# Cross attention of an encoder-decoder layer: VectorE's sums and GpSimd's product of a normalization put in separate slots

## The chip, the core and the metric

The kernel runs on one core of a Trainium2 chip. The metric is the device time of one execution in microseconds (us). Everything is float32. The engines are named as the profile names them: PE (TensorE matmuls), PEld (its weight loads), DVE (VectorE), ACT (ScalarE), POOL (GpSimd) and SP (SyncE, which here only issues DMAs).

## The reference

One encoder layer works on a short context (2 sequences of 77 tokens), and one decoder layer on 2 sequences of 2048 tokens. The width is 512, with 16 heads of 32 and a feed-forward width of 2048. What the change touches is the decoder's cross attention, and what lies beside it is the decoder's feed-forward layer.

```
def _mha(xq, xkv, w_in, b_in, w_out, b_out, bias):
    ...
    scores = jnp.einsum('bhqd,bhkd->bhqk', q, k) / jnp.sqrt(jnp.asarray(hd, xq.dtype))
    scores = scores + bias[None]
    attn = jax.nn.softmax(scores, axis=-1)
    out = jnp.einsum('bhqk,bhkd->bhqd', attn, v)
    ...
    return out @ w_out.T + b_out
...
y = y + _mha(yn, yn, dec_sa_in_w, ...)                       # causal self attention
y = y + _mha(_ln(y, ...), memory, dec_ca_in_w, ..., cb)      # cross attention: 77 keys
h = _ln(y, dec_n3_s, dec_n3_b)
y = y + (jax.nn.relu(h @ dec_ff1_w.T + dec_ff1_b) @ dec_ff2_w.T + dec_ff2_b)
```

## The kernel before

The 4096 decoder rows are cut into eight blocks of 512 tokens (two batches of four), and each block into four query tiles of 128 tokens. The order of the instructions on every engine is written out by hand. No scheduler moves anything: an engine takes its own queue in the order in which the program issues it, and semaphores make it wait for other engines.

The first part of the span (to about 1780 us) is the encoder and the causal self attention of all blocks, with the cross attention of the first block worked in (`first_cross`). In the second part (from about 1780 us to the end) the loop goes over the blocks' feed-forward layers. Each block has 56 slots: 28 for the first weight matrix and 28 for the second. Both products are done by a scheme of seven block products (`PARTS`, `ORDER`) instead of eight, whose operands are sums and differences of quarters of the matrices. Each of the seven takes four slots.

A slot is `ff_slot(s)`. It first calls `prepare(s + 3)`, which builds the operands of the slot three later, and then issues the product of slot s itself (`first_product`, L1132, or `second_product`, L1161). In the first layer POOL builds the sums of weight quarters (L1115, `vv<-pp`) into a ring of four buffers, and sums of activations (`oT<-nT`). In the second layer DVE builds one of the two operands (also L1115). After a product DVE adds it into the result (L1147), and ACT applies the relu (L1150).

While the loop does the feed-forward layer of block x, a generator `cross(x + 1)` issues the cross attention of the next block, one step of a list called `plan` per slot. The step stands ahead of the slot's own `ff_slot`. There are seven such blocks, x = 0 to 6. Query tile t starts at slot 14 + 7t, and its stages are placed at fixed distances from that start:

- `score`: 16 matmuls (L766), then on DVE for each of four groups of heads the maximum (L775) and its subtraction (L776). In the first block of a batch the bias is added ahead of these for tiles 0 and 1 (L773). One of the seven, at about 2280 us in the profile, has this.
- `exp`: one exponential on ACT over 16 x 77 values per row (L779).
- `normalize`: DVE's sum (L784) and reciprocal (L785), and POOL's product of the probabilities with the reciprocals (L786).
- `turned`: 16 transposes on PE (L792), with copies to SBUF on DVE and ACT (L794, L796).
- `times_v`: 16 small matmuls (L803) and a copy on ACT (L807).
- `out`: four matmuls (L812) and DVE's addition into the residual (L813).

For tiles 1 to 3 the six stages stand at distances 0, 2, 3, 6, 9 and 11 from the tile's start. For tile 0 the first three stand one slot earlier, at -1, 1 and 2. So tile 0's score is issued ahead of slot 13, its exponential ahead of slot 15, its normalization ahead of slot 16, and its transposes ahead of slot 20.

Of the kernel before, what the change touches and what calls it, by code (L numbers as in the profile page):

```python
# [54 lines left out]
def tile_encoder_decoder(ctx: ExitStack, tc: tile.TileContext, ins, out):  # L55
# [5 lines left out]
    def wchunk(name, c0, n=D):  # L61

        return ins[name][:, c0 : c0 + n].rearrange("(c p) o -> p c o", p=P)
# [85 lines left out]
    with (  # L149
# [20 lines left out]
        def bank():  # L170

            i = count["bank"] % count["banks"]
            count["bank"] += 1
            return psum[:, i, :]
# [6 lines left out]
        def rows4(r):  # L181
            return slice(r * HD, (r + 1) * HD)
# [571 lines left out]
        def attend_stages(q, kTc, v, y, biased, pr, pts, place, w_o, bi=None):  # L754


            prh = pr.rearrange("p (h k) -> p h k", k=S)
            by_r = pr.rearrange("p (g r k) -> p g r k", r=HC, k=S)
            keep = {}

            def score():
                mx = sm.tile([P, NC, HC], F32, name="cmx", tag="cmx", bufs=3)
                banks = [bank() for _ in range(HC)]
                for g in range(NC):
                    for r in range(HC):
                        nc.tensor.matmul(  # L766
                            banks[r][:, ts(g, S)], q(g)[rows4(r)], kTc[rows4(r), g, :], start=True, stop=True
                        )
                for r in range(HC):
                    s = banks[r][:, : NC * S].rearrange("p (g k) -> p g k", k=S)  # L770
                    d = by_r[:, :, r, :]
                    if biased:
                        nc.vector.tensor_tensor(d, s, bi[r] if bi else d, ALU.add)  # L773
                        s = d
                    nc.vector.tensor_reduce(mx[:, :, r], s, AX.X, ALU.max)  # L775
                    nc.vector.tensor_tensor(d, s, mx[:, :, r, None].to_broadcast([P, NC, S]), ALU.subtract)  # L776

            def exp():
                nc.scalar.activation(pr, pr, AF.Exp)  # L779

            def normalize():
                su = sm.tile([P, H], F32, name="csu", tag="csu", bufs=2)
                ri = sm.tile([P, H], F32, name="cri", tag="cri", bufs=2)
                nc.vector.tensor_reduce(su, prh, AX.X, ALU.add)  # L784
                nc.vector.reciprocal(ri, su)  # L785
                nc.gpsimd.tensor_tensor(prh, prh, ri[:, :, None].to_broadcast([P, H, S]), ALU.mult)  # L786

            def turned():
                for g in range(NC):
                    pt = bank()  # L790
                    for r in range(HC):
                        nc.tensor.transpose(pt[:S, ts(r, P)], prh[:, g * HC + r, :], ident)  # L792
                    if g % 2:
                        nc.vector.tensor_copy(pts(g), pt[:S, :])  # L794
                    else:
                        nc.scalar.copy(pts(g), pt[:S, :])  # L796

            def times_v():
                ot = bank()
                for g in range(NC):  # L800
                    for r in range(HC):
                        h = g * HC + r
                        nc.tensor.matmul(  # L803
                            ot[rows4(r), ts(g, P)], v[:, ts(h, HD)], pts(g)[:, ts(r, P)], start=True, stop=True
                        )
                keep["oT"] = place()
                nc.scalar.copy(keep["oT"], ot)  # L807

            def out():
                mm, oT = bank(), keep["oT"]  # L810
                for c in range(NC):
                    nc.tensor.matmul(mm, oT[:, ts(c, P)], w_o[:, c, :], start=(c == 0), stop=(c == NC - 1))  # L812
                nc.vector.tensor_tensor(y(), mm, y(), ALU.add)  # L813

            return score, exp, normalize, turned, times_v, out

        def first_cross():


            plan = {}  # L820

            def at(slot, f):
                plan.setdefault(slot, []).append(f)

            o = 2 * HC * MB
            ys = [pp[:, o + t * D : o + (t + 1) * D] for t in range(TB)]
            qT = pp[:, o + 2048 : o + 4096].rearrange("p (g n) -> p g n", n=MB)
            prs = [pp[:, o + 4096 + i * H * S : o + 4096 + (i + 1) * H * S] for i in range(2)]
            o += 4096 + 2 * H * S
            kTc = pp[:, o : o + NC * S].rearrange("p (c k) -> p c k", k=S)  # L830
            vc = pp[:S, o + NC * S : o + NC * S + D]
            slab = pp[:, o + NC * S + D : o + NC * S + 2 * D].rearrange("p (c n) -> p c n", n=P)
            assert o + NC * S + 2 * D <= 12288
            nT = pp[:, HC * MB : 2 * HC * MB].rearrange("p (c n) -> p c n", n=MB)
            wq, wo = vv[:, 8:12, :], vv[:, 12:16, :]
            rows = {"dec_ca_out_b": kT[:, 0, 3 * MB :], "dec_ff2_b": kT[:, 3, 3 * MB :]}
            oT, xn = kT[:, 1, 3 * MB :], kT[:, 2, 3 * MB :]

            def pts(g):
                return kT[:S, g, 2 * MB : 3 * MB]  # L840

            def loads():
                for t in range(TB):
                    nc.sync.dma_start(ys[t], y1[0][0][:, t, :])
                for n, row in rows.items():
                    i = _ROWS.index(n)
                    nc.sync.dma_start(row, ins["rows"][i : i + 1, :].to_broadcast([P, D]))
                nc.sync.dma_start(wq, wchunk("dec_ca_in_wT", 0))
                nc.sync.dma_start(kTc, ckT_d[:, :, :S])
                nc.sync.dma_start(vc, cv_d[:, 0, :])  # L850

            def more_loads():
                for i in range(2):
                    bias_tile(prs[i].rearrange("p (h k) -> p h k", k=S), 2, P, S, 255 - P * i)
                nc.sync.dma_start(wo, wchunk("dec_ca_out_wT", 0))

            at(0, loads)
            at(5, more_loads)
            for t in range(TB):
                y = lambda t=t: ys[t]  # L860
                fs = norm_stages(
                    y, "n2", rows["dec_ca_out_b"], lambda: xn, lambda t=t: nT[:, :, ts(t, P)]
                )
                for k, f in enumerate(fs):
                    at(1 + t + k, f)
            for g in range(NC):
                at(7 + g, lambda g=g: q_group(g, wq[:, :, ts(g, P)], nT, qT[:, g, :]))
            for t in range(TB):
                y = lambda t=t: ys[t]
                fs = attend_stages(  # L870
                    lambda g, t=t: qT[:, g, ts(t, P)], kTc, vc, y, t < 2, prs[t % 2], pts, lambda: oT, wo
                )
                for k, f in zip((0, 1, 2, 4, 5, 6), fs):
                    at(11 + 3 * t + k, f)
                fs = norm_stages(y, "n3", rows["dec_ff2_b"], lambda: xn, lambda: slab)
                for k, f in enumerate(fs):
                    at(18 + 3 * t + k, f)

                def store(t=t):
                    nc.sync.dma_start(nT3_d[:, :, ts(t, P)], slab)  # L880
                    nc.sync.dma_start(y1[0][0][:, t, :], ys[t])

                at(20 + 3 * t, store)
            return plan
# [307 lines left out]
        def cross(x):  # L1192
# [9 lines left out]
            for t in range(TB):  # L1202
                fs = norm_stages(
                    lambda t=t: y_of(x, t), "n2", bv, place("xt"), lambda t=t: nT2[:, :, ts(t, P)]
                )
# [11 lines left out]
            for t in range(TB):  # L1217
                at = 14 + 7 * t
                y = lambda t=t: y_of(x, t)
                biased = m == 0 and t < 2  # L1220
                fs = attend_stages(
                    lambda g, t=t: qT[g // 2][:, g % 2, ts(t, P)], kTcs[b], vcs[b][:S, :], y, biased, pr,
                    lambda g: pts_all[:S, g, :], place("xr"), wbt,
                    bias_1 if biased and t else None,
                )

                for k, f in zip((0 if t else -1, 2 if t else 1, 3 if t else 2, 6, 9, 11), fs):
                    plan[at + k].append(f)
                fs = norm_stages(y, "n3", bo, place("xt"), lambda t=t: nTt[:, :, ts(t, P)])
                for k, f in zip((13, 15, 17), fs):  # L1230
                    plan[at + k].append(f)
# [129 lines left out]
```

## Time and profile before

| What | us |
|---|---|
| Time, median of 3 runs | 2927.04 (2926.18 to 2927.46) |
| The profiled execution, its own time | 2926.58 |
| Its span, first to last instruction | 2924.8 |
| PE busy in the span | 2866.0 (98%) |
| DVE busy | 2096.9 (72%) |
| ACT busy | 1303.8 (45%) |
| POOL busy | 744.8 (25%) |
| Mean granted TensorE clock | 0.990 |

The profile is of one execution. A row of a timeline gives the start in us, the duration in us, the engine, the line and operation, the output and inputs with their shapes, the number of instructions merged into the row, and in square brackets how long the engine was idle before it and whose work ended that. A row of waits gives who waited for whom, the total in us, the number of times and the longest. A row of the table of stretches gives, for a stretch of the span, the busy time and count of PE, PEld, DVE, ACT and POOL, then the granted PE clock (PEclk, 1.00 is full), the DMA share and GB/s. PE works on a float32 matmul in two passes, and the trace counts each: four matmuls show as x8.

### The profile page before, as it was taken

What the parts mean: (1) busy time and instruction counts of PE and PEld (TensorE: products, weight loads), DVE (VectorE), ACT (ScalarE), POOL (GpSimd) and SP (SyncE); (2) the same over time, 40 slices, a digit from 0 to 9 for tenths busy, and PEclk for the clock granted to TensorE, in tenths of its full rate; (3) what the DMA queues carried; (4) which work ended last, traced back from release to release, by engine and by line L of the source; (5) the groups of instructions that cost most, each with busy time, mean ns of one, the idle gap of its engine ahead of it and who ended that gap; (6) DMA issues with size and microseconds to landing.
All of it is one profiled execution on the core that took longest, in us unless ns stands there. A gap on an engine that the chain in (4) does not pass through costs nothing.

```text
span 2924.8 us, 60785 instructions
## 1 busy us (share of the span) xinstructions
PE 2866.0 (98%) x24440; PEld 2018.7 (69%) x24440; DVE 2096.9 (72%) x5951; ACT 1303.8 (45%) x2431; POOL 744.8 (25%) x601
## 2 busy tenths in 40 slices
PE   8899999999999999999999999999999999999999
PEld 5557666666666556666666667777777777777788
DVE  4767688888987788888888894646474756565645
ACT  3344456546665445565566673323232323232321
POOL 0100000000000101000000004565656464646464
PEclk9899999999999999999999999999999999999999
DMA  6413301201111502211201115000001000000000
GB/s 176 98 54 112 100 16 54 65 16 45 34 41 60 141 19 73 73 30 48 56 16 37 41 39 198 1 30 1 29 1 47 1 29 1 30 1 30 1 15 15
DMA packets 117837, 137.11 MB, mean 47 GB/s; under 512 B 18433, under 2 KB 73265, under 8 KB 117427
## 3 DMA queue, kind: packets, MB, share of 16 engines
q1 hardware_dynamic: 117554, 133.22, 15.5%
q8 instruction: 192, 3.15, 0.4%
q14 instruction: 91, 0.74, 0.1%
HBM read 111.33 MB, written 21.86 MB: 46 GB/s over the span
## 4 chain that ended last, share of the span: by engine, by line
PE 86%; DVE 11%; issue 1%; ACT 1%; DMA 1%; POOL 0%; SPq 0%; DVEq 0%; POOLq 0%; ACTq 0%
PE psum L1161 13%; PE psum L1132 13%; PE psum L411 12%; PE psum L361 10%; PE psum L428 7%; DVE pp L370 5%; PE psum L206 4%; PE psum L812 4%; PE psum L751 4%; PE psum L230 4%; PE psum L242 4%; PE psum L217 3%; DVE pp L377 3%; PE psum L792 2%; PE psum L766 1%
## 5 line engine op out<-in xcount | busy, mean ns | idle before, releaser
L387 ACT ACTIVATE pp<-pp,nm 128x128 f32<-128x128 f32 (+15 forms) x512 | 614.1, 1210 | 197.7 <-DVE nm L384 194.9
L370 DVE TENSOR_SCALAR_CACHE_REDUCE pp<-psum 128x512 f32<-128x512 f32 (+3 forms) x1024 | 557.9, 589 | 53.5 <-PE psum L361 51.5
L411 PE MATMUL psum<-ident,pp 128*128 128x128 f32 x4352 | 547.9, 279 | 17.6 <-DVE mx L377 11.7
L411 PEld LDWEIGHTS psum<-ident,pp 128*128 128x128 f32 x4352 | 474.2, 142 | 130.3 <-DVE pp L370 56.5
L417 ACT COPY pts<-psum 128x512 f32<-128x512 f32 (+3 forms) x592 | 298.6, 577 | 516.9 <-PE psum L411 390.9
L1115 POOL TENSOR_TENSOR vv<-pp 128x512 f32<-128x512 f32 x320 | 425.3, 1345 | 148.6 <-PE psum L1132 128.5
L361 PE MATMUL psum<-kT,q 32*128 32x512 f32 (+3 forms) x2560 | 351.8, 579 | 8.2 <-DVE mx L377 4.0
L415 DVE COPY pts<-psum 128x512 f32<-128x512 f32 (+2 forms) x544 | 329.7, 659 | 40.7 <-PE psum L411 38.9
L428 PEld LDWEIGHTS psum<-pts,vv 128*32 128x32 f32 x8704 | 226.2, 110 | 124.3 <-issue 116.9
L428 PE MATMUL psum<-pts,vv 128*32 128x128 f32 x8704 | 278.9, 276 | 0.4 <-DVE vv L233 0.4
L1147 DVE TENSOR_TENSOR kT<-kT,psum 128x512 f32<-128x512 f32 x256 | 166.5, 681 | 133.1 <-PE psum L1132 125.9
L276 POOL TENSOR_TENSOR rstd<-rstd,mhalf 128x1 f32<-128x1 f32 x32 | 18.2, 568 | 918.3 <-DVE rstd L275 855.4
L377 DVE CUSTOM_DVE_ANT_0 pp<-psum,bias 128x256 f32<-128x256 f32 (+1 forms) x512 | 209.4, 409 | 24.6 <-PE psum L361 16.7
L361 PEld LDWEIGHTS psum<-kT,q 32*128 32x128 f32 x2560 | 119.5, 184 | 151.8 <-issue 97.7
L1150 ACT ACTIVATE kT<-kT,vecs 128x256 f32<-128x256 f32 x256 | 115.2, 499 | 196.5 <-DVE kT L1147 196.5
L1161 PE MATMUL psum<-vv 128*128 128x256 f32 x768 | 176.9, 381 | 0.0
L1132 PE MATMUL psum<-oT,vv 128*128 128x256 f32 x736 | 166.8, 380 | 1.5 <-POOL vv L1115 1.5
L1161 PEld LDWEIGHTS psum<-vv 128*128 128x128 f32 x768 | 143.1, 190 | 26.8 <-issue 9.5
L1145 ACT COPY kT<-psum 128x512 f32<-128x512 f32 x124 | 69.5, 587 | 204.4 <-DVE kT L1147 133.8
L1132 PEld LDWEIGHTS psum<-oT,vv 128*128 128x128 f32 x736 | 138.7, 190 | 26.2 <-issue 6.2
L1115 DVE TENSOR_TENSOR vv<-kT 128x512 f32<-128x512 f32 x160 | 131.1, 834 | 17.6 <-PE psum L1161 16.6
L1132 PE MATMUL psum<-nT,vv 128*128 128x256 f32 x512 | 122.0, 389 | 15.1 <-POOL vv L1115 14.6
(176 smaller groups left out, 3870.3 us busy)
## 6 DMA issues: line engine op xcount, KB each, us to landing
wqk<-in_dec_sa_in_wT_dram SPq DMA_DIRECT2D x64, 256.0 KB, 3.7
bias<-tz SPq DMA_DIRECT2D x128, 128.0 KB, 3.6
wbig<-in_dec_sa_in_wT_dram SPq DMA_DIRECT2D x8, 1024.0 KB, 8.5
vv<-in_enc_ff_wT_dram SPq DMA_DIRECT2D x8, 1024.0 KB, 5.7
wbig<-in_dec_sa_out_wT_dram SPq DMA_DIRECT2D x8, 1024.0 KB, 7.7
vv<-y SPq DMA_DIRECT2D x32, 256.0 KB, 3.2
out_dram<-vv SPq DMA_DIRECT2D x32, 256.0 KB, 2.0
xt<-in_x_dram SPq DMA_DIRECT2D x30, 256.0 KB, 3.6
```

The costliest lines, as they stand in the source:

```text
L361: nc.tensor.matmul(banks[r][:, : kn * P], q[rows4(r), ts(t, P)], kT[rows4(r), g, k0 * P : (k0 + kn) * P], start=True, stop=True,)
L370: nc.vector.tensor_scalar(p[:, k0 * P : (k0 + far) * P], s[:, : far * P], 1.0, None, ALU.mult, ALU.max, accum_out=st["mx"][:, r, c : c + 1],)
L377: nc.vector.tensor_tensor_reduce(p[:, (i + 1) * P - w : (i + 1) * P], s[:, far * P : kn * P], biases[b, m, g][:, r, 2 * P - w :], 1.0, LOW ...
L387: nc.scalar.activation(p, p, AF.Exp, bias=nm, accum_out=to)
L411: nc.tensor.transpose(pt[:, ts(x, P)], state[n]["p"][r][:, ts(k, P)], ident)
L415: nc.vector.tensor_copy(pts[:, : len(load), :], pt[:, :w])
L417: nc.scalar.copy(pts[:, : len(load), :], pt[:, :w])
L428: nc.tensor.matmul(ot[rows4(r), t, :], vv[:, k, ts(g * HC + r, HD)], got.pop((n, k, r)), start=(k == 0), stop=(k == i),)
L1115: engine.tensor_tensor(dst, quarter(*parts[0], n), quarter(*parts[2], n), SIGN[parts[1]])
L1132: nc.tensor.matmul(mm[:, ts(f, TOK)], a[:, c, ts(f, P)], b[:, c, :], start=(c == 0), stop=(c == 1))
L1147: nc.vector.tensor_tensor(dst, dst, got, SIGN[sign])
L1161: nc.tensor.matmul(mm[:, t, :], lhs[:, c, ts(t, P)], rhs[:, c, :], start=(n == 0 and c == 0), stop=(n == 3 and c == 1),)
```

## The change

`normalize` is split in two. The new stage `sums` holds DVE's sum and reciprocal and leaves the reciprocals in `keep`. `normalize` keeps POOL's product. Seven stages are now placed. For tile 0 of the blocks in the loop the sums stay at distance 2 (slot 16), and the product goes to distance 3 (slot 17). For tiles 1 to 3 and in `first_cross` both stand in one slot, as before.

```
-            def normalize():
+            def sums():
                 su = sm.tile([P, H], F32, name="csu", tag="csu", bufs=2)
                 ri = sm.tile([P, H], F32, name="cri", tag="cri", bufs=2)
                 nc.vector.tensor_reduce(su, prh, AX.X, ALU.add)
                 nc.vector.reciprocal(ri, su)
+                keep["ri"] = ri
+
+            def normalize():
+                ri = keep["ri"]
                 nc.gpsimd.tensor_tensor(prh, prh, ri[:, :, None].to_broadcast([P, H, S]), ALU.mult)
...
-            return score, exp, normalize, turned, times_v, out
+            return score, exp, sums, normalize, turned, times_v, out
...
-                for k, f in zip((0, 1, 2, 4, 5, 6), fs):
+                for k, f in zip((0, 1, 2, 2, 4, 5, 6), fs):
                     at(11 + 3 * t + k, f)
...
-                for k, f in zip((0 if t else -1, 2 if t else 1, 3 if t else 2, 6, 9, 11), fs):
+                for k, f in zip((0, 2, 3, 3, 6, 9, 11) if t else (-1, 1, 2, 3, 6, 9, 11), fs):
                     plan[at + k].append(f)
```

## The prediction

> **What bounds the kernel now.** I read the page's engine rows first, then TensorE's waits in the second half (where the moved step runs seven times), then the order of time of PE, POOL and DVE around one of these waits, and last the granted clock there.
>
> ```profile
> PE 2866.0 (98%) x24440; PEld 2018.7 (69%) x24440; DVE 2096.9 (72%) x5951; ACT 1303.8 (45%) x2431; POOL 744.8 (25%) x601
> ...
> L1132 PE MATMUL psum<-nT,vv 128*128 128x256 f32 x512 | 122.0, 389 | 15.1 <-POOL vv L1115 14.6
> ...
> PE psum L1132 <- POOL vv L1115: 16.1, 7, 4.4
> PE psum L812 <- ACT xr L807: 0.9, 1, 0.9
> PE psum L1132 <- DVE kT L1147: 0.5, 1, 0.5
> ```
>
> PE is the bound: busy 98% of the span. From 1780 us to the end it waits 17.5 us in all, and 16.1 us of that is one kind of wait, seven times: a product of the first feed-forward layer (L1132) for an operand that POOL builds (L1115). Seven is the number of blocks in which the loop carries another block's cross attention. Here is one, in the block at 2130 us: PE, then POOL, then DVE.
>
> ```profile
> 2126.26 5.34 PE L1132 MATMUL psum<-nT,vv 128*128 128x256 f32 x24
> 2133.64 1.99 PE L1132 MATMUL psum<-nT,vv 128*128 128x256 f32 x8 [2.04 <-POOL vv L1115]
> 2135.47 1.91 PE L792 MATMUL psum<-ident,oT 128*77 128x128 f32 x16
> ...
> 2124.84 1.27 POOL L1115 TENSOR_TENSOR vv<-pp 128x512 f32<-128x512 f32 x1 [0.46 <-PE psum L1132]
> 2130.11 2.25 POOL L786 TENSOR_TENSOR oT<-oT,cri 128x1232 f32<-128x1232 f32 x1 [3.99 <-DVE cri L785]
> 2132.31 1.27 POOL L1115 TENSOR_TENSOR vv<-pp 128x512 f32<-128x512 f32 x1
> 2133.54 2.50 POOL L1115 TENSOR_TENSOR oT<-nT 128x512 f32<-128x512 f32 x2
> ...
> 2129.71 0.25 DVE L785 RECIPROCAL cri<-csu 128x16 f32<-128x16 f32 x1
> 2129.88 3.61 DVE L1147 TENSOR_TENSOR kT<-kT,psum 128x512 f32<-128x512 f32 x6
> 2135.67 1.29 DVE L1147 TENSOR_TENSOR kT<-kT,psum 128x512 f32<-128x512 f32 x2 [2.19 <-PE psum L1132]
> ```
>
> A slot's product is four matmuls, x8 rows here. Between the score of query tile 0 (L766, ahead of slot 13) and its transposes (L792, ahead of slot 20) the trace has x24, x24, x8: slots 13 to 19, and the x8 that waited is slot 19. Its operand is built three slots early, in slot 16, and in slot 16 the normalizing product (L786) is issued ahead of it. POOL takes its queue in order: it idles 3.99 us for DVE's reciprocal, spends 2.25 us on L786, and only then 1.27 us on the operand. PE sits 2.04 us behind that.
>
> Last the clock, in the blocks at 1981 (two stretches), 2130 and 2429 us; the column before DMA is PEclk:
>
> ```profile
> 1985.60:1987.60 2.00, 2.00 (x9) 1.55 (x8) 0.00 (x0) 0.00 (x0) 2.00 (x3) 0.68 0.00 0
> 1987.60:1989.60 2.00, 2.00 (x11) 2.00 (x10) 1.35 (x3) 1.05 (x3) 2.00 (x2) 0.50 0.00 0
> 2134.11:2136.11 2.00, 2.00 (x14) 1.78 (x13) 0.44 (x1) 0.00 (x0) 2.00 (x3) 1.00 0.00 0
> 2433.53:2435.53 2.00, 2.00 (x7) 1.53 (x6) 0.00 (x0) 0.00 (x0) 2.00 (x3) 0.50 0.00 0
> ```
>
> In two of the five ordinary blocks with a 2.04 us wait the clock falls to half just after it.
>
> **What the change does.** Every instruction remains. Tile 0's sum and reciprocal (L784, L785) stay in slot 16, so DVE's order is unchanged, and so are the orders of PE, ACT and SP's DMA queue. Tiles 1 to 3, and the four tiles of the first block's own attention (L786 from 1042 us), keep both steps in one slot. Only POOL's queue changes: in each of seven blocks tile 0's L786 moves from slot 16 to slot 17, past one instruction, slot 19's operand. It issues no DMA. No wait disappears from L786; PE's transposes now wait for it directly, where before they came behind slot 19's product and so behind L786 anyway.
>
> **The cost, in the block at 2130 us.** The operand needs its ring buffer (four of them), which slot 15's product frees. That product ends at 2126.26; L1115 started 0.3 us after such a release, so it runs 2126.6 to 2127.9, in POOL's idle 3.99 us. L786 still starts at 2130.11, when the reciprocal is there, and ends at 2132.36. PE finishes slot 18 at 2131.60 and goes on at once with slot 19, to 2133.4: the transposes find L786 done 1.0 us earlier (0.8 if the weight load's lead of 0.2 is counted). Slot 20's operand (the first of the oT<-nT pair, 1.25 us) now follows L786 directly and ends near 2133.6; PE wants it at 2137.22 - 2.04 = 2135.18. So PE gains the whole 2.04 us.
>
> What is late next? DVE's queue: its six L1147 end at 2133.49, and the pair for slot 19 would be wanted at 2135.67 - 2.04 = 2133.63. Its 2.19 us of idle shrinks to 0.14, but stays above zero. ACT's L1150 pair follows DVE with its own idle. After that PE has no wait in this block on the page's list, and DVE idles about 1 us in most slots, so nothing takes the time back. I cost moving the operand at 0: POOL's idle covers it; without that cover it would delay L786 by 1.27, of which 0.8 is hidden.
>
> **Clock.** Between L786 of tile 0 and of tile 1 the undisturbed blocks take 20.25 us (2130.11 to 2150.36). At 1981.60 it is 21.92, at 2429.53 it is 21.94: 1.67 and 1.69 us more, about half of the 3.4 us or so spent at 0.5. The Trainium skill (TensorE: Matmul & The Clock Gate, HAM oscillation) asks for no TensorE gap above about 3.4 us; a 2.04 us gap would be harmless by it, and this 3.4 us would not be the gap's doing. The trace shows the drop directly behind the gap in two of five, so I take it as its price: with the rule the sum below is 15.5, with the trace 18.9.
>
> **The block with a bias (2280 us)** differs. There PE waits 4.44 us, since DVE adds the bias before the maximum (L773) and the reciprocal comes late against PE. With the operand early, PE runs slot 19 from 2279.1 to 2280.9 and then must wait for L786, to 2282.3: 1.4 to 1.5 us of the stall stays, now before the transposes. Then a second point, against the change. L776 takes 0.48 us as a rule, but 1.23 at 2270.34, beside a POOL operand that began at 2269.96, and 0.79 at 2272.50. The Trainium skill (SBUF — State Buffer, SBUF: two separate sides) says why: a VectorE operation with two SBUF inputs and a GpSimd one that reads SBUF exclude each other. In this block alone L776 has both inputs in SBUF; in the others it reads PSUM, and stays at 0.48 beside POOL. The moved operand would run at about 2273.4 to 2274.7, on top of the last L776 (2274.23): about 0.46 us, between 0 and 0.75, on the way to the reciprocal. With DVE and ACT as they follow (six L1147, then the pair, then the copies before the next score), the next score starts at 2286.4 to 2287 where it was 2290.50. That includes the half clock of 2282 to 2287, which I expect gone with a stall of 2 us instead of 4.4. I take 3.8 us gained; without the port 4.3; if the clock still falls, 2.1.
>
> **Sum.** First block (1834 us): 1.52, at full clock. Three ordinary blocks at full clock: 2.04 + 2.04 + 2.03 = 6.11. Two with the clock drop: 2.04 + 1.67 + 2.03 + 1.69 = 7.43. Bias block: 3.8. Together 18.9 us. The profiled execution took 2926.58 us (span 2924.8 and 1.8 around it), 0.46 below the median 2927.04. 2926.58 - 18.9 = 2907.7; with the 0.46, 2908.2 for a median.
>
> **Rivals.** *Part is given back* (0.15): DVE's remaining 0.14 us is too thin, the copies L794/L796 come late, and the score behind them waits 0.5 to 1 us in six blocks; or the clock drops elsewhere. Against it: ACT and DVE copies ended 0.7 us or more before that score. Gain 13 to 16: 2910.5 to 2914.
>
> *The stall only moves to the transposes* (0.03), as in the bias block, everywhere: L786 would have to end 0.8 us later and more. Needs 2 us more to cancel the gain: 2922 to 2927, within 0.2%. Against it: L786 is tied to the reciprocal, which is untouched.
>
> *Slower* (0.03): the operand's buffer is not free when its turn comes, and L786 queues behind it. If slot 18 rather than 15 frees it (at 2131.60), the operand ends at 2133.2, L786 at 2135.4, and the transposes start where they did: no gain. That is the point from which it decides; each PE slot later is 1.73 us, in seven blocks 12 us: 2939. Against it: POOL's operands at 2123.12 and 2124.84 start a slot apart, each behind the product four slots back.
>
> **How the numbers follow.** The likeliest case, the whole stall returned, has 0.79: 2905.5 to 2910, its width from the clock drops (1.7 each) and the bias block (2.1 to 4.3). The range takes in the second case to 2913. What a measurement of this kernel can tell from no change is about 0.2%, 5.9 us. The first two cases are faster by more than that (0.94), the third is the same, the fourth slower.
>
> **What would show it.** Right: no PE wait for L1115 but in no or one block; POOL's operand near 2126.6 before L786; some 2.2 us of POOL idle left before L786, until the reciprocal; a PE wait of 1.4 to 2 us before L792 in the bias block alone; clock 1.00 in all ordinary blocks after slot 19. Wrong: PE waits before L792 or L766 in ordinary blocks, or POOL's operand starting after 2130.

## The result, and the profile after

The changed kernel takes 2906.32 us (median of 5, 2904.86 to 2907.74) where the kernel before, measured beside it, takes 2926.99 us (2925.14 to 2927.46). The ratio is 0.9931, with a 95% interval of 0.9916 to 0.9945: 20.7 us, or 0.7%, faster. The forecast was 2908.2 us, with cases from 2905.5 to 2913.

The changed kernel has four more lines ahead of the product, so L1132, L1115, L786, L792, L807, L812 and L1147 of before are L1136, L1119, L790, L796, L811, L816 and L1151 now. The page's engine row, and all of TensorE's waits in the feed-forward part (1780 us to the end):

```profile
PE 2858.3 (98%) x24440; PEld 2012.6 (69%) x24440; DVE 2101.7 (72%) x5951; ACT 1304.3 (45%) x2431; POOL 742.8 (26%) x601
...
PE psum L796 <- POOL oT L790: 1.5, 1, 1.5
PE psum L816 <- ACT xr L811: 0.9, 1, 0.9
PE psum L1136 <- DVE kT L1151: 0.8, 1, 0.8
```

The wait that was 16.1 us in seven pieces is gone from the list. One new wait of 1.5 us stands ahead of the transposes, in the block with a bias, and the short wait for DVE in that block is 0.8 us where it was 0.5. The block that the prediction followed, in the timeline after, PE, then POOL, then DVE:

```profile
2121.89 7.07 PE L1136 MATMUL psum<-nT,vv 128*128 128x256 f32 x32
2128.79 1.91 PE L796 MATMUL psum<-ident,oT 128*77 128x128 f32 x16
...
2122.20 1.28 POOL L1119 TENSOR_TENSOR vv<-pp 128x512 f32<-128x512 f32 x1 [0.45 <-PE psum L1136]
2125.74 2.25 POOL L790 TENSOR_TENSOR oT<-oT,cri 128x1232 f32<-128x1232 f32 x1 [2.27 <-DVE cri L785]
2127.95 2.50 POOL L1119 TENSOR_TENSOR oT<-nT 128x512 f32<-128x512 f32 x2
...
2125.34 0.25 DVE L785 RECIPROCAL cri<-csu 128x16 f32<-128x16 f32 x1
2125.52 4.81 DVE L1151 TENSOR_TENSOR kT<-kT,psum 128x512 f32<-128x512 f32 x8
2130.24 1.27 DVE L798 COPY pts<-psum 77x512 f32<-77x512 f32 x2
```

PE's x24 and the x8 that waited are now one row of x32: slots 16 to 19 without a break. POOL builds slot 19's operand right behind the release of its buffer, idles 2.27 us (before 3.99), and runs the product when the reciprocal is there, as before. The product ends at 2127.99, 0.8 us ahead of the transposes. DVE's six additions and the two of slot 19 are one row of x8: its 2.19 us of idle is used up, and PE waits for nothing because of it.

Two executions differ by some us before the second part begins: the first score of the loop (L766) starts at 1825.1 us in the profile before, 1826.5 after, and 1824.3 to 1828.2 over the experiments. So I compare profiles from that point to the span's end, and block by block from the start of tile 0's product to that of tile 1's, which both stand in POOL's timeline:

| us, by block (start about) | 1835 | 1981 | 2126 | 2274 (bias) | 2419 | 2563 | 2708 | first score to end |
|---|---|---|---|---|---|---|---|---|
| before | 20.22 | 21.92 | 20.25 | 23.75 | 21.94 | 20.25 | 20.25 | 1099.73 |
| after | 18.44 | 17.95 | 17.95 | 19.24 | 17.95 | 17.95 | 17.95 | 1078.87 |
| less | 1.78 | 3.97 | 2.30 | 4.51 | 3.99 | 2.30 | 2.30 | 20.86 |

The seven differences add up to 21.15 us. In the bias block 0.31 us is lost again ahead of tile 0's product (from the previous block's tile 1 product to it: 130.00 us, before 129.69). 21.15 - 0.31 = 20.84 us, all of the gain.

### The profile page after: what moved, and what is told of

Same layout as the page of the kernel before. It is cut to its first block, busy times and chain, and to the rows that moved or that the text cites. A ratio compares the mean times of both kernels' runs of the same rounds, so it can differ in the third digit from the quotient of the medians.

```text
span 2905.3 us, 60785 instructions
## 1 busy us (share of the span) xinstructions
PE 2858.3 (98%) x24440; PEld 2012.6 (69%) x24440; DVE 2101.7 (72%) x5951; ACT 1304.3 (45%) x2431; POOL 742.8 (26%) x601
## 4 chain that ended last, share of the span: by engine, by line
PE 86%; DVE 11%; issue 1%; ACT 1%; DMA 1%; POOL 0%; SPq 0%; DVEq 0%; ACTq 0%; POOLq 0%
PE psum L1165 14%; PE psum L1136 13%; PE psum L411 12%; PE psum L361 10%; PE psum L428 7%; DVE pp L370 5%; PE psum L230 4%; PE psum L206 4%; PE psum L816 4%; PE psum L751 4%; PE psum L242 4%; PE psum L217 3%; DVE pp L377 3%; PE psum L796 2%; PE psum L766 1%; PE psum L807 1%
## 5 line engine op out<-in xcount | busy, mean ns | idle before, releaser
L1119 POOL TENSOR_TENSOR vv<-pp 128x512 f32<-128x512 f32 x320 | 421.7, 1334 | 153.6 <-PE psum L1136 133.8
L1151 DVE TENSOR_TENSOR kT<-kT,psum 128x512 f32<-128x512 f32 x256 | 166.0, 680 | 113.2 <-PE psum L1136 107.8
L1136 PE MATMUL psum<-oT,vv 128*128 128x256 f32 x736 | 166.5, 380 | 0.0
L1136 PEld LDWEIGHTS psum<-oT,vv 128*128 128x128 f32 x736 | 138.8, 190 | 24.4 <-issue 6.2
L1119 DVE TENSOR_TENSOR vv<-kT 128x512 f32<-128x512 f32 x160 | 134.1, 853 | 14.5 <-PE psum L1165 13.6
L257 POOL TENSOR_TENSOR xr<-xr,row_dec_sa_out_b 128x512 f32<-128x512 f32 x30 | 38.1, 1271 | 372.9 <-DMA xr<-in_x_dram 302.4
```

What stands on the lines that cost most here:

```text
L1119: engine.tensor_tensor(dst, quarter(*parts[0], n), quarter(*parts[2], n), SIGN[parts[1]])
L1136: nc.tensor.matmul(mm[:, ts(f, TOK)], a[:, c, ts(f, P)], b[:, c, :], start=(c == 0), stop=(c == 1))
L1151: nc.vector.tensor_tensor(dst, dst, got, SIGN[sign])
```

## The experiments

The theory: POOL's order alone is the cause, one instruction past another, block by block; the gain is the idle of PE, the half clock behind it, and something fixed per wait that the idle does not show. The rivals: a chain between blocks, the place of the sums, or luck with the clock. Where a cut shows only the tuple of a line that changes, the rest of the line is left out.

**One block undone.** The change in six blocks, the old place in the bias block.

```
-                for k, f in zip((0, 2, 3, 3, 6, 9, 11) if t else (-1, 1, 2, 3, 6, 9, 11), fs):
+                first = (-1, 1, 2, 2 if m == 0 else 3, 6, 9, 11)
+                for k, f in zip((0, 2, 3, 3, 6, 9, 11) if t else first, fs):
```

> The change in six of the seven blocks; in the block whose tile 0 has a bias the product goes back to slot 16, ahead of slot 19's operand. Theory (the order of product and operand on POOL is the whole cause, block by block): only that block changes. There PE waits about 4.4 us before slot 19 again and no longer before the transposes, the fourth subtraction of the score (L776) falls from 0.79 to 0.48 us and the product starts about 0.3 us earlier against the score; from this block's product to tile 1's it is 23.75 us again if the clock falls and about 22.1 if not, in place of 19.24. In all 2.5 to 4.3 us more than the changed kernel: 2909 to 2911, while the other six blocks keep 17.95 us (18.44 in the first). Rival (part of the gain comes from a chain between blocks, the later ones being early because the earlier ones are): the other blocks' distances move too.

Measured: 2912.49 us (ratio to before 0.9949, 0.9935 to 0.9964). The other six blocks kept 18.43 and 17.94 to 17.95. In the undone block PE waits 4.45 us before slot 19 again, and the distance is 24.57 us in place of 19.24. The blocks are independent; the rival falls. The size was missed: 5.4 us from the first score to the end (1084.2), where 2.5 to 4.3 was expected. The clock is what was longer: 0.50 in three stretches in a row, from before PE resumed at 2278.40. The half clock lasts 6.83 us in the trace, 4.8 us of it behind the wait, where the kernel before had 3.41 us with 3.1 behind it. Half of these 1.7 us more is about the 0.82 us between 24.57 and the forecast 23.75.

```profile
2277.00:2279.00 2.00, 0.60 (x2) 0.51 (x3) 1.26 (x3) 1.31 (x4) 2.00 (x3) 0.50 0.00 0
2279.00:2281.00 2.00, 2.00 (x6) 1.64 (x5) 0.00 (x0) 0.00 (x0) 2.00 (x3) 0.50 0.00 0
2281.00:2283.00 2.00, 2.00 (x8) 1.65 (x8) 0.78 (x2) 0.06 (x1) 2.00 (x2) 0.50 0.00 0
```

The last subtraction is back at 0.48 us and the product 0.3 us earlier against the score, as expected, yet the stretch up to the product took 130.04 us and not 129.69. The trace puts these 0.35 us ahead of the score, at 2233 to 2240 us, where VectorE waited 1.93 us for a normalization's load (L726, `vv<-y`); after the change it waited 0.52. In the runs below with 1.64 and 1.50 us at this load, TensorE lost 0.25 and 0.18 us at the same place, so the loss goes with the wait for the load. That the load is its cause is not shown.

**The product one slot later still.**

```
-  (-1, 1, 2, 3, 6, 9, 11)
+  (-1, 1, 2, 4, 6, 9, 11)
```

> The change with the product one slot later still: tile 0's product in slot 18, behind slot 20's operand too. Theory: the product waits for the reciprocal anyway, and slot 20's operand (1.25 us) fits into POOL's idle 2.3 us before it, so the five ordinary blocks and the first stay as with the change (17.95 and 18.44 us from tile 0's product to tile 1's) and the time is 2906 within 1.5 us; in the bias block the second POOL operand may hold the last subtraction of the score longer, 0 to 1.3 us more there. Rival (it matters how late in the program the product stands): the transposes wait for the product in the ordinary blocks, about 1.2 us in each, 2912.

Measured: 2906.68 us (0.9930, 0.9915 to 0.9945), every block as after the change within 0.01 us (18.43, 17.94 to 17.95, 19.24). Two operands now stand in POOL's idle, and the product still starts behind the reciprocal:

```profile
2121.96 1.28 POOL L1119 TENSOR_TENSOR vv<-pp 128x512 f32<-128x512 f32 x1 [0.45 <-PE psum L1136]
2123.20 1.27 POOL L1119 TENSOR_TENSOR oT<-nT 128x512 f32<-128x512 f32 x1
2125.51 2.25 POOL L790 TENSOR_TENSOR oT<-oT,cri 128x1232 f32<-128x1232 f32 x1 [1.04 <-DVE cri L785]
```

So it did not matter that the product stood a slot later in the program, only what stood in front of it and whether that was done before the reciprocal. In the bias block the extra operand cost nothing: DVE's last subtraction took 0.79 us, as after the change, and the operand that began beside it took 1.51 us in place of 1.27.

**The sums late too.** Sums and product both in slot 17.

```
-  (-1, 1, 2, 3, 6, 9, 11)
+  (-1, 1, 3, 3, 6, 9, 11)
```

> The whole normalization of tile 0 in slot 17: the sums move too, behind VectorE's additions of slot 16. Theory (the split's two halves do different things: the product's place frees slot 19's operand, the sums' place keeps the reciprocal early): the reciprocal comes about 1.2 us later in the five ordinary blocks, the product ends about 1.2 us later and the transposes wait 0.3 to 0.5 us for it; 0.3 to 0.7 us lost in each of five blocks, nothing in the bias block (where the exponential, not the additions, holds the sums) and nothing in the first; 2908 to 2910. Rival (the sums' place is indifferent): 2906, no wait before the transposes but in the bias block.

Measured: 2907.86 us (0.9933, 0.9916 to 0.9949), just under the 2908 to 2910 expected; from the first score to the end 1081.1, 2.3 us more than after the change. From tile 1's product to the next block's it is 145.0 us where it was 144.54 to 144.56 (behind the bias block 144.1, where it was 143.7); the bias block keeps 149.25. PE waits for the product in six blocks, 2.6 us in all:

```profile
PE psum L796 <- POOL oT L790: 2.6, 6, 1.5
...
2129.09 2.25 POOL L790 TENSOR_TENSOR oT<-oT,cri 128x1232 f32<-128x1232 f32 x1 [3.40 <-DVE cri L785]
...
2131.39 1.97 PE L796 MATMUL psum<-ident,oT 128*77 128x128 f32 x16 [0.22 <-POOL oT L790]
```

Keeping the sums in slot 16 is worth these 2.3 us in the profile; the times alone, 1.5 us apart with overlapping intervals, do not tell it. Each wait shows 0.22 us and costs 0.45.

**A shorter and a longer wait.** Both start from the kernel before, with its order. The first multiplies half the heads of tile 0 and leaves the others without their normalization, the second multiplies half of them twice. The added lines shift the line numbers by one and by three.

```
+                n = H // 2 if tile0 else H
-                nc.gpsimd.tensor_tensor(prh, prh, ri[:, :, None].to_broadcast([P, H, S]), ALU.mult)
+                nc.gpsimd.tensor_tensor(prh[:, :n], prh[:, :n], ri[:, :n, None].to_broadcast([P, n, S]), ALU.mult)
...
                 nc.gpsimd.tensor_tensor(prh, prh, ri[:, :, None].to_broadcast([P, H, S]), ALU.mult)
+                if tile0:
+                    n = H // 2
+                    nc.gpsimd.tensor_tensor(prh[:, :n], prh[:, :n], ri[:, :n, None].to_broadcast([P, n, S]), ALU.mult)
```

> The kernel before, with the order as it was, but tile 0's product in the seven blocks multiplies only the first 8 of 16 heads (heads 8 to 15 of that tile stay without their normalization). The product takes about 1.15 us instead of 2.25. Theory: the operand behind it is 1.1 us earlier, so PE's waits shrink to 0.94 in five blocks, 0.4 in the first and 3.3 in the bias block; 7 x 1.1 = 7.7 us, and the half clock after the wait does not come (3.4 us) in the ordinary blocks: 2915.5 to 2919.5. If a wait has a fixed cost beside the idle that the trace shows (0.26 us by the difference of before and after), it stays here, since every wait stays: 19.15 us from product to product in the ordinary blocks, that is 17.95 + 0.94 + 0.26 us. Rival (the idle shown is the whole cost): 18.9. Rival on the clock (the drop is unrelated to the length of the wait): it still falls in one to three blocks, 1.7 us each.

> The kernel before, in its old order, with the first 8 heads of tile 0's product multiplied a second time in the seven blocks (those probabilities come out scaled twice): about 1.18 us more POOL work ahead of slot 19's operand. Theory (PE's wait follows POOL's queue one for one, and the clock falls more often the longer the wait): waits of about 3.2 us in five blocks, 2.7 in the first and 5.6 in the bias block, 7 x 1.18 = 8.3 us more than before; from product to product 21.4 us at full clock and 23 to 24 with a drop, and a drop in four or five of the five ordinary blocks where the kernel before had two: 2937 to 2943. Rival (a gap below 3.4 us leaves the clock alone, the two drops of before are something else): no more drops than before in the ordinary blocks, 2935.

Measured: 2916.99 us (0.9967, 0.9956 to 0.9979) and 2943.11 us (1.0053, 1.0038 to 1.0068), the second 0.1 us over what was expected. The waits, first with half the product, then with one and a half, and the slot 19 of one block in each:

```profile
PE psum L1133 <- POOL vv L1116: 8.9, 7, 3.4
...
2129.22 1.99 PE L1133 MATMUL psum<-nT,vv 128*128 128x256 f32 x8 [1.00 <-POOL vv L1116]
2131.05 1.91 PE L793 MATMUL psum<-ident,oT 128*77 128x128 f32 x16
```

```profile
PE psum L1135 <- POOL vv L1118: 25.2, 7, 5.7
...
2141.09 2.93 PE L1135 MATMUL psum<-nT,vv 128*128 128x256 f32 x8 [3.32 <-POOL vv L1118]
2143.82 2.69 PE L795 MATMUL psum<-ident,oT 128*77 128x128 f32 x16
...
2142.00:2145.00 3.00, 3.00 (x12) 2.46 (x11) 0.94 (x2) 0.22 (x1) 3.00 (x4) 0.50 0.00 0
```

PE's idle follows POOL's queue nearly one for one: 1.00, 2.04 and 3.32 us for a product of 1.22, 2.25 and 2.25 + 1.22. The distances in the six blocks without a bias make a scale of what a wait costs:

| PE idle shown, us | blocks | distance, us | over 17.95 and the idle | reading |
|---|---|---|---|---|
| 0 (after) | 5 | 17.95 | 0 | |
| 1.00 (half product) | 5 | 19.22 | 0.27 | full clock |
| 2.04 (before) | 3 | 20.25 | 0.26 | full clock |
| 2.04 (before) | 2 | 21.92, 21.94 | 1.93, 1.95 | clock fell |
| 3.32 (longer product) | 5 | 23.21 to 23.23 | 1.94 to 1.96 | clock fell, all five |

So a wait ahead of slot 19 has a fixed price of 0.26 us beside its idle, and a drop of the clock costs 1.67 to 1.70 us more. It fell in 0 of 5, 2 of 5 and 5 of 5 blocks.

Length alone does not decide, since the five waits of 2.04 us are alike. Their place in time does. In the traces every half clock from the first score on lasts 3.41 us or 6.83, but for a rest at the very end, and the starts in one run lie whole multiples of 3.413 us apart: 1986.30, 2283.26 and 2433.45 us before (87 and 44 times), and seven starts with the longer product (44 or 45 times). Cut the span into cells of 3.413 us along these starts. Here are the cell with the 2.04 us wait at 1983 us and the one behind it, then the two cells that share the 2.04 us wait at 2132 us, in the kernel before:

```profile
1982.89:1986.30 3.41, 1.38 (x6) 1.06 (x6) 2.09 (x4) 1.86 (x5) 3.41 (x4) 1.00 0.00 0
1986.30:1989.71 3.41, 3.41 (x14) 3.05 (x13) 1.46 (x3) 1.16 (x3) 3.41 (x3) 0.50 0.00 0
2129.66:2133.07 3.41, 1.94 (x9) 1.36 (x8) 3.38 (x8) 1.96 (x5) 2.96 (x2) 1.00 0.01 2
2133.07:2136.48 3.41, 2.84 (x18) 2.59 (x19) 1.23 (x3) 0.85 (x3) 3.41 (x4) 1.00 0.00 0
```

The two 2.04 us waits that lost the clock lie whole in one cell. The three that kept it are cut by a cell's edge, into 1.47 and 0.56, 0.68 and 1.36, and 0.61 and 1.42 us. Over the runs with a half clock in this part, a cell with 2.03 us of waiting or more was always followed by one at half clock, and a cell at full clock with 1.52 us or less never; nothing lies between. At half clock less was enough to keep it: 2.06, 1.21 and 1.82 us of waiting in such a cell (in the bias block, with the change undone there, with half and with the longer product) were followed by another cell at half, which is how those half clocks came to 6.83 us. No run moved the cells on purpose, so this is read from the traces and not tested by an experiment. In the first block, measured from 18.44, a 1.52 us wait kept the clock and a 2.81 us wait lost it. The rival, that a gap below 3.4 us leaves the clock alone, falls: it gave 2935 us for the longer product. In the bias block the half product gained nothing in distance (23.94 us, before 23.75): PE waited 3.41 us there, cut by a cell's edge into 2.20 and 1.21. The clock was at 0.50 already when it resumed and stayed there for 6.83 us in place of 3.41, so about 1 us less idle was paid back in slow matmuls.

**The exponential early in the bias block**, added to the change.

```
-  (-1, 1, 2, 3, 6, 9, 11)
+  (-1, -1 if m == 0 else 1, 2, 3, 6, 9, 11)
```

> The change, and in the bias block tile 0's exponential straight behind its score (slot 13 in place of 15), ahead of ScalarE's relus of slots 13 and 14. Theory (in that block VectorE's sums wait for the exponential, which waits in ScalarE's queue behind relus that nobody needs yet): VectorE's idle of 1.70 us before the sums goes, the product starts about 1.6 us earlier, PE's remaining 1.49 us before the transposes goes, with the fixed 0.26; about 1.7 us less than the changed kernel, 2904.6, the other blocks as they are. Rival (VectorE's queue, full in that block, is the bound behind it): the wait before the transposes goes and comes back at the output projection, whose wait grows from 0.86 to about 2.4 us; 2906.

**The change again**, on the chip of the run with the early exponential:

> The changed kernel once more, on the same chip as the two others: 2906 within 1.5 us, no PE wait before slot 19 in any block, 17.95 us from tile 0's product to tile 1's in the five ordinary blocks, 18.44 in the first and 19.24 in the bias block. Whatever differs between two executions of it then lies ahead of 1800 us, in the start. Rival (part of its gain was one execution's luck with the clock): half clock in some block of the second part, 1.7 us more there.

Measured: 2905.07 us (0.9923, 0.9911 to 0.9936) with the early exponential, 2906.65 us (0.9929, 0.9916 to 0.9941) without. The change repeats: every block as in the first profile, 18.43, 17.94 to 17.96 and 19.24, and 1078.9 us from the first score to the end, without half clock in between, so no luck with the clock. With the early exponential VectorE's idle of 1.70 us before the sums is gone, and so is PE's wait; these are the only waits left in the second part:

```profile
PE psum L816 <- ACT xr L811: 0.9, 1, 0.9
PE psum L1136 <- DVE kT L1151: 0.8, 1, 0.8
...
2266.44 1.23 ACT L779 ACTIVATE oT<-oT 128x1232 f32<-128x1232 f32 x1 [6.54 <-POOL vv L1119]
...
2268.07 1.43 DVE L784 TENSOR_REDUCE csu<-oT 128x16 f32<-128x1232 f32 x1
...
2272.36 1.91 PE L796 MATMUL psum<-ident,oT 128*77 128x128 f32 x16
```

From the first score to the end it takes 1077.3 us, 1.5 us less than the change, where 1.7 was expected. At the transposes themselves TensorE gains 1.71 us, the wait of 1.49 and 0.22 beside it; 0.18 us went ahead of that, at 2236 us, where the load named above came late. The wait at the output projection stays at 0.86, against the rival. This is the fastest of the profiles, but the two medians are 1.6 us apart with overlapping intervals, so the step beyond the change rests on the profile.

## Why the prediction was right, point by point

- *POOL's queue.* The operand needed only its buffer, the product only the reciprocal, and each got what it needed without the other. The operand started 0.31 us behind the release (counted from slot 16's start, as in the prediction), the product right behind the reciprocal, as forecast. The experiment with the product in slot 18 shows that the cover was as large as worked out.
- *The margin of the transposes* was forecast at 1.0 us to the matmuls and 0.8 to their weight load. It is 0.80 us to the matmuls (2128.79 against 2127.99) and 0.59 to the weight load at 2128.58, 0.2 us less, since TensorE arrives earlier by the price of a wait that the sum left out. Putting the sums one slot later made the product 1.1 us later, used the margin up and started to wait.
- *DVE's margin* of 0.14 us was too fine to call. With the real gain of 2.30 us it was spent: DVE runs without a break from the reciprocal to the copies. It cost nothing, because the copies end at 2131.51, ahead of the next score at 2132.36, and DVE idles again from there. The rival that gives part back did not come.
- *The clock.* It stayed at full in every ordinary block, and the two blocks gave back 1.67 and 1.69 us beyond the others, the figures of the sum. The 15.5 us that the gap rule would have given is short of the measured gain by 5. Two drops are the count of the one profiled execution, whose 2926.58 us lay near the median. The prediction had no reason why two and not another number, so that this count fits the medians is in part luck.
- *The bias block.* The remaining wait was 1.49 us (forecast 1.4 to 1.5), before the transposes as said. The port cost 0.31 us in place of 0.46: the last subtraction took 0.79. The block gave 4.20 us (4.51 - 0.31) against 3.8; the clock did not fall there.
- *A slip in a rival.* A gain of 13 to 16 us would have given 2911 to 2914 us, not 2910.5 to 2914. Nothing hangs on it.
- *The term that was too small* is the price of a wait. The sum took the idle that the trace shows, 2.04 us, and put what a wait costs beside it at nothing; the profile shows 2.30 returned. In the first and the five ordinary blocks that is 6 x 0.26 = 1.6 us, and with 0.4 us in the bias block the 18.9 of the sum becomes 20.9.

## What to carry to other kernels

On an engine with an in-order queue, look for an instruction that waits long for another engine and has ready work of the bound engine queued behind it; let the ready work pass, and leave the waiting one's own trigger where it is. Before moving it, write down what it must still precede, and by how much: here 0.8 us, less than the 1.1 us by which later sums delayed the product. Price a wait of the bound engine by two equal stretches of program, with and without it, not by the idle alone.

## What the hardware showed that was not expected

A TensorE wait cost more here than the idle that the profile shows: 0.26 us more ahead of slot 19, 0.22 and 0.23 ahead of the transposes (1.71 for 1.49, 0.45 for 0.22). In the timeline before, slots 16 to 18 are x24 with an end at 2126.26 + 5.34 = 2131.60 (the profile models the ends of matmuls); in the unbroken row after, 32 matmul rows lead to the next start 6.90 us later (2121.89 to 2128.79), so 24 take 5.18, and the next product would have begun at 2131.44. The product behind the wait then takes 1.83 us to the next start (2133.64 to 2135.47) where an unbroken one takes 1.73. The 0.16 us between modelled end and next start and the 0.10 us of a slower product make the 0.26.

The clock did not need one long gap either: 2.03 us of waiting inside one cell of 3.413 us halved it for the next 3.41 us, while waits of 2.04 us that a cell's edge cut in two left it at full.
